# Other addresses for the stationary operands of a cross-attention, and value products that walk backwards

## The chip, the core and the metric

The kernel runs on one core of a Trainium2 chip. The metric is the device time of one execution in microseconds. Two runs of the kernel before took 585.60 and 587.18 us, median 586.39.

## What is computed

A block of 256 tokens (width 512) attends to 25,088 context rows, then runs a small causal self-attention and a mixture of eight experts. Nearly all of the time goes into the cross-attention:

```python
qp = einsum('bsd,ed->bse', q, Wq) + bq        # 256 x 128
kp = einsum('bsd,ed->bse', k, Wk) + bk        # 25088 x 128
vp = einsum('bsd,ed->bse', v, Wv) + bv        # 25088 x 512
z  = sigmoid(einsum('bqe,bke->bqk', qp, kp) / sqrt(128))
return einsum('bqk,bkd->bqd', z, vp)
```

There is no softmax, so the order can be turned round: the kernel sums z times the raw context rows, and multiplies the 256 x 512 result by Wv at the end (the bias bv enters with the row sums of z).

## The kernel before

**Numbers.** Each float32 operand of these products is split in two float32r parts, hi and lo (`split`, lines 62 to 65: ACT casts, DVE or POOL subtracts). `mm3` (lines 67 to 70) makes a product of three: hi x hi, hi x lo, lo x hi, added up in one bank of PSUM. The profile's lines L68, L69 and L70 are these three, wherever they are called from, so products are told apart by their tiles.

**Stationary and moving.** A product on TensorE has a stationary operand (`lhsT`, 128 columns here), which is loaded into the array first, and a moving operand (`rhs`), whose columns stream through. The profile shows the load as LDWEIGHTS on a row of its own, PEld, beside the running product on PE.

**The chunk loop.** The context comes in 49 chunks of 512 rows, each in two layouts: transposed (`rT`) and natural (`rN`), 1 MB each, loaded by SP's queue two or three chunks ahead. For each chunk:

- key products (`kp_mm`): stationary `wk` (four blocks j), moving the split transposed chunk T; 4 x 3 products of 512 columns
- scores (`scores`, two pairs of key tiles): stationary the chunk's `kp`, moving `qp`; 12 products of 256 columns. ACT applies the sigmoid, DVE adds z to its running sum, and z is split
- value products (`av`): for each of four key tiles t and two token halves q: stationary a 128 x 128 block of z, moving 512 columns of N (the split natural chunk), added up in `acc0` or `acc1`; 4 x 2 x 3 products of 512 columns

In TensorE's order the key products of the next chunk come first, then the value products of tiles 0 and 1, a score group of the next chunk, value products of tile 2, another score group, and those of tile 3. The order on each engine is the order of the program text (`in_order` fixes it). Beside this, `prepare` splits other weights and writes them to DRAM, a piece per chunk. After the loop come the 256-row stages, in a sequence written out by hand.

**Places in SBUF.** Tiles come from two pools, `sm` and then `sb`, placed one after the other in order of first request. In the program before, `half` is 41 columns wide instead of 1. All tiles in question begin at a multiple of 256 bytes, and so do the blocks taken from them: for every float32r product, stationary and moving operand lie at 0 modulo 256 bytes. `wk` are two tiles of 512 columns in `sb`; a `z` tile is [128, 2, 256], four buffers for each of hi and lo.

Of the kernel before, what the change touches and what calls it, by code (L numbers as in the profile page):

```python
# [11 lines left out]
F32 = mybir.dt.float32  # L12
F32R = mybir.dt.float32r
BF16 = mybir.dt.bfloat16
# [6 lines left out]
P = 128  # L21
T = 256
D = 512
KD = D // P
# [3 lines left out]
NT = CK // P  # L28
E = 8
NH = 16  # L30
LAG = 2
# [17 lines left out]
def body(ctx, tc, a, out, nch=NCH):  # L49
    nc = tc.nc  # L50
# [3 lines left out]
    sm = ctx.enter_context(tc.tile_pool(name="sm", bufs=1))  # L54
    sb = ctx.enter_context(tc.tile_pool(name="sb", bufs=1))
# [3 lines left out]
    def f(t):  # L59
        return t.bitcast(F32)  # L60

    def split(hi, lo, src, eng=nc.vector):

        copy(hi, src)  # L64
        eng.tensor_tensor(lo, src, f(hi), ALU.subtract)  # L65

    def mm3(ps, ahi, alo, bhi, blo, first, last):
        mm(ps, lhsT=ahi, rhs=bhi, start=first, stop=False)  # L68
        mm(ps, lhsT=ahi, rhs=blo, start=False, stop=False)  # L69
        mm(ps, lhsT=alo, rhs=bhi, start=False, stop=last)  # L70

    def pair(name, shape, tag=None, bufs=1):
        return [sb.tile(shape, F32R, tag=f"{tag or name}{i}", name=f"{name}_{i}", bufs=bufs) for i in range(2)]

    def bank(name):
        return psum.tile([P, D], F32, tag="b", name=name, bufs=6)
# [4 lines left out]
    def toks(t):  # L81
        return slice(t * P, (t + 1) * P)


    ident = sm.tile([P, P], F32, name="ident")
    make_identity(nc, ident)
    half = sm.tile([P, 41], F32, name="half")[:, 0:1]
    nc.gpsimd.memset(half, -0.5)
    ones = sm.tile([P, 1], F32, name="ones")
    nc.gpsimd.memset(ones, 1.0)  # L90
    x_sb = [sb.tile([P, D], F32, tag=f"x{t}", name=f"x_sb{t}") for t in range(2)]
    bq = sm.tile([P, 1], F32, name="bq")
    bk = sm.tile([P, 1], F32, name="bk")
    bv = sb.tile([P, D], F32, name="bv")
    rows = sm.tile([P, 2], F32, name="rows")
    zacc = sb.tile([P, 2, T], F32, name="zacc")
    nc.vector.memset(zacc, 0.0)
    wv = pair("wv", [P, KD * D], "wvo")
# [1 line left out]


    plain = {"wkvd": D, "wqr": 4 * 64, "wkr": 64, "wku": D, "wvu": D, "wq2": KD * D, "gate": KD * E}
    pw = {n: (sb if w % P == 0 else sm).tile([P, w], F32, name=n) for n, w in plain.items()}
    plain = list(pw)
    spill = {n: dram.tile([P, 2 * w], F32, name=f"sp_{n}") for n, w in (("wo", KD * D), ("gu", E * 2 * D), ("dn", E * D))}

    todo = [("wv", at, None, at) for at in range(0, KD * D, D)]
# [2 lines left out]
    todo += [("wo", at, KD * D, at) for at in range(0, KD * D, D)]  # L110


    mask = sm.tile([P, P], BF16, name="mask")
    nc.gpsimd.memset(mask, 0.0)
    nc.gpsimd.affine_select(out=mask, in_=mask, compare_op=ALU.is_ge, fill=MASKED, base=0, pattern=[[-1, P]],
                            channel_multiplier=1)
# [5 lines left out]
    def moments(x, tag):  # L122
        s6 = sm.tile([P, nc.vector.BN_STATS_DIM], F32, tag="s6", name=f"s6{tag}", bufs=2)
        mv = sm.tile([P, 2], F32, tag="mv", name=f"mv{tag}", bufs=2)
        rs = sm.tile([P, 1], F32, tag="rs", name=f"rs{tag}", bufs=2)
        nc.vector.bn_stats(s6, x)
        nc.vector.bn_aggr(mv, s6)
        nc.vector.tensor_scalar(rs, mv[:, 1:2], 1e-5, None, ALU.add)
        nc.gpsimd.tensor_tensor(rs, rs, half, ALU.pow)
        return mv, rs  # L130
# [12 lines left out]
    rT, rN, sT, sN, kp, zz = {}, {}, {}, {}, {}, {}  # L143
# [24 lines left out]
    def kp_mm(c, blocks=range(KD)):  # L168
        th, tl = sT[c]
        if c not in kp:  # L170
            kp[c] = bank(f"kp_ps{c}")
        ps = kp[c]
        for j in blocks:
            mm3(ps, wk[0][:, toks(j)], wk[1][:, toks(j)], th[:, j, :], tl[:, j, :], j == 0, j == KD - 1)

    def kp_out(c):
        ps, kp[c] = kp[c], pair(f"kp{c}", [P, CK], "kp", 2)
# [3 lines left out]
    def scores(c, p):  # L181
        ps = bank(f"sc{c}_{p}").rearrange("p (i t) -> p i t", i=2)
        for i in range(2):
            t = toks(2 * p + i)
            mm3(ps[:, i, :], kp[c][0][:, t], kp[c][1][:, t], qp[0], qp[1], True, True)
        z = sb.tile([P, 2, T], F32, tag="z", name=f"z{c}_{p}", bufs=2)
        nc.scalar.activation(z, ps, AF.Sigmoid, scale=1.0 / math.sqrt(128.0))  # L187
        zz[c, p] = pair(f"z{c}_{p}", [P, 2, T], "z", 2 * LAG)
        tt2(zacc, zacc, z, ALU.add)  # L189
        split(*zz[c, p], z)  # L190

    def av(c, t, q):
        zh, zl = zz[c, t // 2]
        nh, nl = sN[c]
        mm3(acc[q], zh[:, t % 2, toks(q)], zl[:, t % 2, toks(q)], nh[:, t, :], nl[:, t, :],
            c == 0 and t == 0, c == nch - 1 and t == NT - 1)

    def prepare(n):

# [12 lines left out]
    def load_split(n, tag):  # L212
        r = sb.tile([P, D], F32, tag="wr", name=f"{n}_r", bufs=2)
        nc.sync.dma_start(r, a[n])
        return r, pair(n, [P, D], tag)

    wk_r, wk = load_split("wk", "wk")
    for t in range(2):
        nc.sync.dma_start(x_sb[t], a["x"][:, t, :])
    wq_r, wq = load_split("wq", "at")  # L220
# [8 lines left out]

    acc = [psum.tile([P, D], F32, tag=f"acc{q}", name=f"acc{q}") for q in range(2)]  # L230
    xh, xl = pair("xa", [P, KD, T], "oh")
    warm = sm.tile([P, 1], F32, name="warm")
    nc.scalar.activation(warm, half, AF.Sigmoid)
    split(*wk, wk_r, nc.gpsimd)
    m = [moments(x_sb[tt], f"a{tt}") for tt in range(2)]
    xn = [normal(x_sb[tt], m[tt], f"xa{tt}") for tt in range(2)]
    split(*wq, wq_r, nc.gpsimd)
# [1 line left out]
    for j in range(2):  # L239
        split_T(0, [j])  # L240
        split(xh[:, :, toks(j)], xl[:, :, toks(j)], xps[j])
    split_T(0, [2, 3], nc.gpsimd)
    kp_mm(0, [0, 1])
    qp = pair("qp", [P, T])
    ps = bank("qp_ps")[:, :T]
    for j in range(KD):
        mm3(ps, wq[0][:, toks(j)], wq[1][:, toks(j)], xh[:, j, :], xl[:, j, :], j == 0, j == KD - 1)
    kp_mm(0, [2, 3])
    split_T(1, [0, 1])
    split_T(1, [2, 3], nc.gpsimd)  # L250
    nc.scalar.activation(qp[0], ps, AF.Identity, bias=bq)
    nc.vector.scalar_tensor_tensor(qp[1], ps, bq, f(qp[0]), ALU.add, ALU.subtract)
    kp_out(0)
    split_N(0, [0, 1])
    kp_mm(1, [0, 1])
    scores(0, 0)
    scores(0, 1)
    split_N(0, [2, 3])
    kp_mm(1, [2, 3])
# [3 lines left out]
    for c in range(nch):  # L263
# [23 lines left out]
        for t in range(NT):  # L287
            for q in now:
                av(c, t, q)
            if nx and t in (1, 2):  # L290
                scores(c + 1, t - 1)
        if c >= 4 and plain:
            n = plain.pop()
# [263 lines left out]
    def AV1(n):  # L557
        for _ in range(min(n, len(late))):
            av(*late.pop(0), 1)
# [5 lines left out]
    ps = bank("rows_ps")  # L565
# [54 lines left out]
    Q(1, 2)  # L620
    Q(1, 3)
    ft = sb.tile([P, 2 * D], F32R, tag="wq2", name="ft").rearrange("p (n b e d) -> p n b e d", n=2, b=2, e=2)
    fr, fq = (sb.tile([P, 2, 2, P], F32, tag=f"wk{i}", name=f"f{i}") for i in range(2))
    yhl = pair("y", [P, KD, T], "oh")
    PV(0, 2)
    PV(0, 3)
# [144 lines left out]
```

## Time and profile before

| | |
|---|---|
| median of the runs (2) | 586.39 us |
| profiled execution, its own time | 586.28 us |
| its span, first to last instruction | 584.5 us |
| granted TensorE clock | 1.00 |
| ACT cast of T, 128x2048 | 1.91 us |
| DVE subtraction for T, 128x2048 | 2.29 us |
| rT load of 1 MB, issue to landing | 5.5 us (median) |

How to read it: the busy row gives each engine's busy time; for TensorE the products overlap in the pipeline, so their lengths add up to more than the time that passes. The distance between two starts in the timeline is the pace. In a steady chunk, from 300.86 to 310.50 us, DVE is busy 8.25 us, ACT 7.37 us, and the DMA engines 86%:

```
us, PE busy (x) PEld busy (x) DVE busy (x) ACT busy (x) POOL busy (x), PEclk, DMA share, GB/s
300.86:310.50 9.64, 9.64 (x50) 8.19 (x48) 8.25 (x9) 7.37 (x8) 0.00 (x0) 1.00 0.86 306
```

The page's names for what the change touches: `kp_ps<-T,wk` (key products), `sc<-qp,kp` (scores), `acc<-N,z` (value products), `wk<-wk_r` (split of wk).

### The profile page before, as it was taken

To read this page: it belongs to the slowest core of one execution; us is meant where nothing else is said; L and a number is where in the kernel's file an instruction comes from. 1 tells how busy PE (TensorE), PEld (TensorE's weight loads), DVE (VectorE), ACT (ScalarE), POOL (GpSimd) and SP (SyncE) were. 2 spreads that over 40 slices of the span, in tenths; PEclk is the share of its full clock that TensorE was granted. 3 is DMA by queue.
4 is the path that set the end of the run, shared out by engine and by line. 5 is a ranking of instruction groups with operands and counts; after the bars stand their busy time and mean duration, and the time that the engine had idled before them with its cause. 6 is when DMAs were issued, how large, how long until landed. Compare 5 with 4: busy or idle time off the path is not lost.

```text
span 584.5 us, 8061 instructions
## 1 busy us (share of the span) xinstructions
PE 570.6 (98%) x3036; PEld 481.7 (82%) x3036; DVE 459.7 (79%) x528; ACT 395.1 (68%) x512; POOL 21.1 (4%) x28
## 2 busy tenths in 40 slices
PE   4999999999999999999999999999999999999997
PEld 3888888888888888888888888888888887876996
DVE  6898888888888888888888888787878765667543
ACT  5877777777777777777777776767676752574211
POOL 5200000000000000000000000000000041000000
PEclk9999999999999999999999999999999999999999
DMA  8897887879888888788988887565657477700000
GB/s 288 334 368 283 278 295 281 321 278 317 287 324 276 325 271 325 266 337 298 332 282 319 274 337 245 208 225 206 234 198 243 149 295 262 316 1 1 1 1 36
DMA packets 33526, 144.94 MB, mean 248 GB/s; under 512 B 4240, under 2 KB 4432, under 8 KB 19792
## 3 DMA queue, kind: packets, MB, share of 16 engines
q1 hardware_dynamic: 33488, 144.44, 69.3%
q8 instruction: 23, 0.38, 0.2%
q14 instruction: 15, 0.12, 0.1%
HBM read 129.22 MB, written 15.20 MB: 247 GB/s over the span
## 4 chain that ended last, share of the span: by engine, by line
PE 95%; DVE 3%; DMA 1%; issue 0%; POOL 0%; ACT 0%; SPq 0%; POOLq 0%
PE acc L68 15%; PE acc L69 15%; PE acc L70 15%; PE kp_ps L70 8%; PE kp_ps L69 8%; PE kp_ps L68 8%; PE sc L70 4%; PE sc L69 4%; PE sc L68 4%; PE s L428 2%; PE gu L68 1%; PE gu L69 1%; PE gu L70 1%; PE pt L445 1%; DMA wq_r<-in_wq 1%; PE pv L456 1%
## 5 line engine op out<-in xcount | busy, mean ns | idle before, releaser
L68 PE MATMUL acc<-N,z 128*128 128x512 f32 x392 | 153.9, 393 | 0.0
L69 PE MATMUL acc<-N,z 128*128 128x512 f32 x392 | 153.7, 392 | 0.0
L65 DVE TENSOR_TENSOR N<-rN,N 128x2048 fp32r<-128x2048 f32 (+1 forms) x53 | 111.6, 2110 | 52.3 <-ACT N L64 52.2
L70 PE MATMUL acc<-N,z 128*128 128x512 f32 x392 | 152.5, 389 | 0.0
L65 DVE TENSOR_TENSOR T<-rT,T 128x2048 fp32r<-128x2048 f32 (+1 forms) x49 | 110.3, 2252 | 15.3 <-ACT T L64 15.3
L187 ACT ACTIVATE z<-sc 128x512 f32<-128x512 f32 x98 | 58.7, 599 | 66.5 <-PE sc L70 66.2
L64 ACT CAST N<-rN 128x2048 fp32r<-128x2048 f32 (+1 forms) x55 | 94.4, 1725 | 6.1
L64 ACT CAST T<-rT 128x2048 fp32r<-128x2048 f32 (+1 forms) x55 | 94.3, 1721 | 0.9 <-DMA rT<-in_ctxT 0.7
L70 PEld LDWEIGHTS acc<-N,z 128*128 128x128 f32 x392 | 73.6, 188 | 16.0
L68 PEld LDWEIGHTS acc<-N,z 128*128 128x128 f32 x392 | 74.0, 189 | 12.3
L69 PEld LDWEIGHTS acc<-N,z 128*128 128x128 f32 x392 | 74.0, 189 | 11.7
L68 PE MATMUL kp_ps<-T,wk 128*128 128x512 f32 x196 | 76.9, 392 | 0.0
L70 PE MATMUL kp_ps<-T,wk 128*128 128x512 f32 x196 | 76.7, 392 | 0.0
L69 PE MATMUL kp_ps<-T,wk 128*128 128x512 f32 x192 | 74.7, 389 | 0.0
L189 DVE TENSOR_TENSOR zacc<-zacc,z 128x512 f32<-128x512 f32 x98 | 67.2, 686 | 3.7 <-ACT z L187 1.7
L65 DVE TENSOR_TENSOR z<-z,z 128x512 fp32r<-128x512 f32 x98 | 67.3, 686 | 0.0
L64 ACT CAST z<-z 128x512 fp32r<-128x512 f32 x98 | 61.0, 623 | 3.1
L178 ACT ACTIVATE kp<-kp_ps,bk 128x512 fp32r<-128x512 f32 x49 | 33.9, 691 | 39.9 <-PE kp_ps L70 39.9
L70 PE MATMUL sc<-qp,kp 128*128 128x256 f32 x196 | 55.8, 285 | 0.1
L69 PE MATMUL sc<-qp,kp 128*128 128x256 f32 x196 | 55.4, 283 | 0.0
L68 PE MATMUL sc<-qp,kp 128*128 128x256 f32 x196 | 54.9, 280 | 0.0
L68 PEld LDWEIGHTS kp_ps<-T,wk 128*128 128x128 f32 x196 | 37.1, 189 | 7.8
(177 smaller groups left out, 658.5 us busy)
## 6 DMA issues: line engine op xcount, KB each, us to landing
rN<-in_ctxN SPq DMA_DIRECT2D x49, 1024.0 KB, 5.7
rT<-in_ctxT SPq DMA_DIRECT2D x47, 1024.0 KB, 5.5
sp_gu<-w_gu SPq DMA_DIRECT2D x32, 256.0 KB, 4.3
gu<-sp_gu SPq DMA_DIRECT2D x8, 1024.0 KB, 6.0
r_gu<-in_gu SPq DMA_DIRECT2D x16, 256.0 KB, 5.7
sp_dn<-w_dn SPq DMA_DIRECT2D x16, 256.0 KB, 4.3
dn<-sp_dn SPq DMA_DIRECT2D x16, 256.0 KB, 6.0
r_dn<-in_dn SPq DMA_DIRECT2D x8, 256.0 KB, 6.1
```

The lines of the kernel that those rows point to most:

```text
L64: copy(hi, src)
L65: eng.tensor_tensor(lo, src, f(hi), ALU.subtract)
L68: mm(ps, lhsT=ahi, rhs=bhi, start=first, stop=False)
L69: mm(ps, lhsT=ahi, rhs=blo, start=False, stop=False)
L70: mm(ps, lhsT=alo, rhs=bhi, start=False, stop=last)
L178: nc.scalar.activation(kp[c][0], ps, AF.Identity, bias=bk)
L187: nc.scalar.activation(z, ps, AF.Sigmoid, scale=1.0 / math.sqrt(128.0))
L189: tt2(zacc, zacc, z, ALU.add)
L428: mm(p3[:, h - h0:h - h0 + 2, :], lhsT=qs[:, tt, h // 2, g, :], rhs=kbd[g // 2][:, g % 2, h:h + 2, :nk], start=tt == 1, stop=tt == 0 and h ...
L445: nc.tensor.transpose(ps[:, toks(i * (tt + 1) + kt)], pr[tt, u][:, i, toks(kt)], ident)
L456: mm(pv[tt][r, g, :], lhsT=vs[kt][:, g * P + r.start:g * P + r.stop], rhs=pt[tt, u][:, toks(i * (tt + 1) + kt)], start=kt == 0, stop=kt == tt)
```

## The change

Three things.

1. `wk` moves to `sm`, in two tiles of 568 columns; its four blocks begin at columns 4, 148, 292 and 436, so each lies 64 bytes further modulo 256 than the one before. It is split block by block.
2. A `z` tile gets 16 columns more, and z begins at column 4. With 2112 bytes a buffer, each of the four buffers lies 64 bytes further modulo 256.
3. `mm3` gets `back`: moving operand and output are read and written from the last column to the first. `av` sets it for odd key tiles.

The small tiles are requested in another order (`half` and `pad` 8 columns each), and `fr` and `fq`, which take the place of `wk` after the loop, become views of the wider tiles.

The addresses in the built programs, modulo 256 bytes:

| product | stationary before | moving before | stationary after | moving after | distance after |
|---|---|---|---|---|---|
| key, blocks j = 0 to 3 | 0 | 0 | 48, 112, 176, 240 | 64 | 240, 48, 112, 176 |
| value, by buffer of z | 0 | 0 | 16, 80, 144, 208 | 64 (backwards: from 60) | 208, 16, 80, 144 |
| scores | 0 | 0 | 64 | 64 | 0 |

```diff
-    def mm3(ps, ahi, alo, bhi, blo, first, last):
+    def mm3(ps, ahi, alo, bhi, blo, first, last, back=False):
+        if back:
+            ps, bhi, blo = ps[:, ::-1], bhi[:, ::-1], blo[:, ::-1]
         mm(ps, lhsT=ahi, rhs=bhi, start=first, stop=False)
...
+    ones, bq, bk, warm = [sm.tile([P, 1], F32, name=n) for n in ("ones", "bq", "bk", "warm")]
+    rows = sm.tile([P, 2], F32, name="rows")
+    mask = sm.tile([P, P], BF16, name="mask")
+    wkp = [None, None]
+    wkp[0] = sm.tile([P, D + 56], F32R, tag="wk0", name="wk0")
+    plain = {"wkr": 64}
+    pw = {n: sm.tile([P, w], F32, name=n) for n, w in plain.items()}
+    half = sm.tile([P, 8], F32, name="half")[:, 0:1]
+    wkp[1] = sm.tile([P, D + 56], F32R, tag="wk1", name="wk1")
+    pad = sm.tile([P, 8], F32, name="pad")
     ident = sm.tile([P, P], F32, name="ident")
     make_identity(nc, ident)
-    half = sm.tile([P, 41], F32, name="half")[:, 0:1]
...
-            mm3(ps, wk[0][:, toks(j)], wk[1][:, toks(j)], th[:, j, :], tl[:, j, :], j == 0, j == KD - 1)
+            mm3(ps, wk[0][j], wk[1][j], th[:, j, :], tl[:, j, :], j == 0, j == KD - 1)
...
-        zz[c, p] = pair(f"z{c}_{p}", [P, 2, T], "z", 2 * LAG)
+
+        zz[c, p] = [t[:, 4:2 * T + 4].rearrange("p (i t) -> p i t", i=2)
+                    for t in pair(f"z{c}_{p}", [P, 2 * T + 16], "z", 2 * LAG)]
...
-            c == 0 and t == 0, c == nch - 1 and t == NT - 1)
+            c == 0 and t == 0, c == nch - 1 and t == NT - 1, t % 2 == 1)
...
-    wk_r, wk = load_split("wk", "wk")
+    wk_r = sb.tile([P, D], F32, tag="wr", name="wk_r", bufs=2)
+    nc.sync.dma_start(wk_r, a["wk"])
+
+    wk = [[t[:, o:o + P] for o in (4, 148, 292, 436)] for t in wkp]
...
-    split(*wk, wk_r, nc.gpsimd)
+    for j in range(KD):
+        split(wk[0][j], wk[1][j], wk_r[:, toks(j)], nc.gpsimd)
...
-    fr, fq = (sb.tile([P, 2, 2, P], F32, tag=f"wk{i}", name=f"f{i}") for i in range(2))
+    fr, fq = (sm.tile([P, D + 56], F32, tag=f"wk{i}", name=f"f{i}")[:, 0:D].rearrange("p (b e d) -> p b e d", b=2, e=2)
+              for i in range(2))
```

More of the change, by code (lines that the diff above doesn't have):

```diff
@@ L82, in toks @@
         return slice(t * P, (t + 1) * P)
+    ones, bq, bk, warm = [sm.tile([P, 1], F32, name=n) for n in ("ones", "bq", "bk", "warm")]
[8 more added lines that the diff above has]
+    pad = sm.tile([P, 8], F32, name="pad")
     ident = sm.tile([P, P], F32, name="ident")
     make_identity(nc, ident)
-    half = sm.tile([P, 41], F32, name="half")[:, 0:1]
     nc.gpsimd.memset(half, -0.5)
-    ones = sm.tile([P, 1], F32, name="ones")
     nc.gpsimd.memset(ones, 1.0)
     x_sb = [sb.tile([P, D], F32, tag=f"x{t}", name=f"x_sb{t}") for t in range(2)]
-    bq = sm.tile([P, 1], F32, name="bq")
-    bk = sm.tile([P, 1], F32, name="bk")
     bv = sb.tile([P, D], F32, name="bv")
-    rows = sm.tile([P, 2], F32, name="rows")
     zacc = sb.tile([P, 2, T], F32, name="zacc")
@@ L102, in body @@
     plain = {"wkvd": D, "wqr": 4 * 64, "wkr": 64, "wku": D, "wvu": D, "wq2": KD * D, "gate": KD * E}
-    pw = {n: (sb if w % P == 0 else sm).tile([P, w], F32, name=n) for n, w in plain.items()}
-    plain = list(pw)
+    pw.update({n: (sb if w % P == 0 else sm).tile([P, w], F32, name=n) for n, w in plain.items() if n not in pw})
+    plain = list(plain)
     spill = {n: dram.tile([P, 2 * w], F32, name=f"sp_{n}") for n, w in (("wo", KD * D), ("gu", E * 2 * D), ("dn", E * D))}
@@ L110, in body @@
     todo += [("wo", at, KD * D, at) for at in range(0, KD * D, D)]
-    mask = sm.tile([P, P], BF16, name="mask")
     nc.gpsimd.memset(mask, 0.0)
@@ L231, in body @@
     xh, xl = pair("xa", [P, KD, T], "oh")
-    warm = sm.tile([P, 1], F32, name="warm")
     nc.scalar.activation(warm, half, AF.Sigmoid)
-    split(*wk, wk_r, nc.gpsimd)
+    for j in range(KD):
+        split(wk[0][j], wk[1][j], wk_r[:, toks(j)], nc.gpsimd)
     m = [moments(x_sb[tt], f"a{tt}") for tt in range(2)]
```

## The prediction, on record before the result

> **What bounds the kernel now.** I read the page first: the busy row and the chain of waits, then the groups by cost.
>
> ```profile
> span 584.5 us, 8061 instructions
> PE 570.6 (98%) x3036; PEld 481.7 (82%) x3036; DVE 459.7 (79%) x528; ACT 395.1 (68%) x512; POOL 21.1 (4%) x28
> PE 95%; DVE 3%; DMA 1%; issue 0%; POOL 0%; ACT 0%; SPq 0%; POOLq 0%
> L68 PE MATMUL acc<-N,z 128*128 128x512 f32 x392 | 153.9, 393 | 0.0
> ```
>
> TensorE is the chain: 95% of the span, and its groups have no idle time before them. No wait can be removed to any profit; only the pace of the products counts. The mean of 393 ns is the length of one product in flight and overlaps the next, so the pace has to be read from starts, in the timeline of TensorE. One turn of the chunk loop (300.86 to 310.50 us), with lines left out:
>
> ```profile
> 303.35 0.39 PE L70 MATMUL acc<-N,z 128*128 128x512 f32 x1
> 303.58 0.28 PE L68 MATMUL sc<-qp,kp 128*128 128x256 f32 x1
> ...
> 304.29 0.40 PE L68 MATMUL acc<-N,z 128*128 128x512 f32 x1
> ...
> 305.68 0.28 PE L68 MATMUL sc<-qp,kp 128*128 128x256 f32 x1
> ...
> 307.78 0.39 PE L68 MATMUL kp_ps<-T,wk 128*128 128x512 f32 x1
> ...
> 310.50 0.39 PE L68 MATMUL acc<-N,z 128*128 128x512 f32 x1
> ```
>
> The twelve key products take 307.78 to 310.50, so 226.7 ns each. The six score products (256 columns) take 0.71 us, 118 ns each. The six value products after a score group take 1.39 us, 231.7 ns each, five ns more than the twelve before 303.58. A chunk is 48 products in 9.64 us, and 49 chunks make 472 of the 584.5 us.
>
> How near is that to the least possible? Three products elsewhere in the trace answer, again by the distance of starts:
>
> ```profile
> 13.25 0.41 PE L69 MATMUL qp_ps<-xa,wq 128*128 128x256 f32 x1
> 13.46 0.41 PE L70 MATMUL qp_ps<-xa,wq 128*128 128x256 f32 x1
> ...
> 506.00 0.38 PE L426 MATMUL s<-mask,identb 128*128 128x512 bf16 x1
> 506.01 0.41 PEld L428 LDWEIGHTS s<-kbd,qs 128*128 128x128 f32 x2
> 506.22 0.38 PE L428 MATMUL s<-kbd,qs 128*128 128x256 f32 x1
> ...
> 513.10 1.06 PE L354 MATMUL q_ps<-xT,wq 128*128 128x128 f32 x8
> 513.99 0.38 PE L426 MATMUL s<-mask,identb 128*128 128x512 bf16 x1
> ```
>
> A 512-column bf16 product lets the next start after 0.22 us (216 ns in the trace's ns), although a float32 stationary operand is loaded beside it. At the start, at half pace, a 256-column float32r product takes 0.21 us, which is 256 columns at 1.2 per ns with nothing added. A plain float32 product of 128 columns comes every 0.89/8 = 111 ns, about the time of its load of 128 columns. So an excess of 226.7 - 216 = 10.7 ns stands only where float32r columns (4 bytes) move at full pace while a load of 4-byte columns runs beside them: 9.6 bytes/ns moving (2048 bytes in 213 ns) against 4.6 loading (512 in 111). It varies too: 114 ns for the first score product of a group and 120 for the later ones, 226.7 or 231.7 for value products of one shape. A fixed price per product would not do that. I read it as the two reads of SBUF disturbing each other. In the program before, every float32r operand lies at 0 modulo 256 bytes, so every distance is 0 and the trace can't show what a distance does.
>
> **What the Trainium skill says.** "TensorE: Matmul & The Clock Gate", section "Wait — 56ns, not 53.3ns?", gives N columns over 2.4 GHz plus about 2.5 ns: 215.7 for 512. The trace agrees for the bf16 product (216), not for float32r (226.7). Its section "Step-by-step: what each phase is for" says that TensorE has two independent read ports and that a load doesn't steal read bandwidth from the running product. If so, a distance can't matter; the 10.7 ns speak against it. "SBUF — State Buffer", section "Door 1: The DMA port swizzle", gives lines of 16 bytes in SBUF and 8 bytes in PSUM, and says that any non-contiguous access to PSUM slows products significantly. No product of before walks backwards, so the trace doesn't test whether a step of -1 counts as such.
>
> **The change part by part.** The order on every engine is as before, except that the split of wk is four casts and four subtractions instead of one each.
>
> *Distances.* 588 key products (49 x 12) and 1176 value products (49 x 24) get distances of 16, 48, ... 240 bytes. Scores keep 0. From both sides: at best the whole excess goes, 1764 x 10.7 = -18.9 us, and with it the extra after score groups, 2 x 6 x 5 ns x 47 chunks = -2.8. At worst it doubles: +18.9. For the value I take: in the 111 ns of a load the load walks 512 bytes and the moving operand 1024, so it gains 512 bytes, twice round 256, from whatever distance it starts. The number of meetings is two at every distance. I take 0.
>
> *Walking backwards.* 588 value products (odd tiles) read and write from the last column. Then the two walks go against each other: 1024 + 512 = 1536 bytes, six times round instead of two. Each meeting is a third as long. If a meeting costs by its length, 0; if each costs the same 5.35 ns, 6 x 5.35 instead of 10.7: +21.4 ns x 588 = +12.6 us. If the reversed order is refused the full pace, a product takes the 430 ns of a plain float32 one (two of them between 521.17 and 522.03): +203 x 588 = +119. Below nothing: at best its own excess goes, which is counted above. I take a quarter of the meeting price, +5.4 ns x 588 = +3.2 us.
>
> *Split of wk.* ACT: a cast of 128 columns isn't shown; between 128x1 (0.20) and 128x512 (0.62) it is about 0.31, so 1.22 instead of 0.62, ending near 4.6 us. ACT's next work, the cast of wq, waits for its DMA until 7.17: hidden. POOL: between 0.55 (one column) and 1.27, about 0.73 each, 2.9 instead of 1.27, from 3.7 to 6.6. Behind it on POOL stands rsa (5.34), which DVE needs at 7.04: with its 0.55 it ends near 7.15. At most +0.5 us; I take 0, since the second rsa starts at 7.20 anyway.
>
> *Moved addresses.* All other tiles start at 64 modulo 256 instead of 0, and each queue issues the same transfers in the same order. "DMA: Bandwidth & Descriptors", section "How a descriptor splits into AXI transactions", charges an unaligned start part of a transaction more. The cover: the rT load issued at 306.42 lands in about 5.5 us and is cast at 321.44, so 9.5 us are spare. If it were gone, ACT's cast of T would wait first. ACT and DVE do the same work on the same shapes; they are busy 7.4 and 8.3 of each 9.64 us. I take 0.
>
> *Sum.* 0 + 3.2 + 0 + 0 = +3.2 us on the profiled execution of 586.28 (span 584.5 and 1.8 around it), which stands at the median, 586.39: 589.5, rounded to **589**.
>
> **The rivals.**
> (a) Distance 0 is the bad one: stationary and moving walks start together, and an odd multiple of 16 bytes keeps them out of each other's lines. For it: the excess changes with the moment of the load (114 against 120). Against: two meetings at any distance. All of the excess and the extra: 586.3 - 18.9 - 2.8 = 565; half of it, 575. DVE's 8.3 us still fit under a chunk of 9.2.
> (b) Slower: distance 0 is the good one, because the walks start in one place and part at once, and other distances add a meeting in the middle of the load. Place: key and value products. Price: double excess, 1764 x 10.7 = +18.9, so 605. It decides from 6.7 ns per product (11.7 us, 2%), or 20 ns on the backward ones alone. For it: the first score product of a group costs 6 ns less than the later ones at distance 0, so cheaper states exist there.
> (c) Reversed columns lose the full pace: 586.3 + 119 = 705. For it: the skill's line on PSUM. Against: a pair of neighbours still fills an 8-byte line in either direction.
> (d) The change does nothing: the ports are independent and the 10.7 ns belong to float32r itself. 586. The varying gaps speak against it.
>
> **How the numbers follow.** The forecast (near-neutral, 583 to 596) 0.35, with (d) 0.10 more: 0.45 within 2% (574.7 to 598.1, about what a measurement of this kernel can tell from no change). (a) 0.20. (b), with the full price of meetings on the backward walk, 0.28, and (c) 0.07: 0.35 slower. The range reaches down to nearly all of (a), 567, and up past (b), 609; (c) and the ends of (a) and (b) are left out.
>
> **What would show it.** In the timeline of TensorE: key products still 226 to 228 ns apart and score products 120 (right: distance is neutral); backward value products 0 to 21 ns above forward ones of the same chunk. Key products near 216 mean (a), near 237 mean (b), backward ones near 430 (c). ACT waiting for rT would show that the transfers lost their cover. I am wrong if the pace of key products moves by more than 3 ns on average, or the backward ones by more than 10.

## The result, and the profile after

The kernel after takes 594.74 us (median of two runs, 594.24 to 595.23), against 586.39 before: a ratio of 1.0148, interval 1.0131 to 1.0164. The change costs 8.35 us, less than 2% but clearly more than nothing. The profiled execution took 594.24 us, 7.96 more than that of before, at the same granted clock of 1.00.

The page of the kernel after: span, busy row, shares of the chain, and the first group by cost (busy us and mean ns of one, then the idle time before it).

```profile
span 592.2 us, 8067 instructions
PE 578.9 (98%) x3036; PEld 481.3 (81%) x3036; DVE 459.6 (78%) x528; ACT 394.9 (67%) x515; POOL 21.6 (4%) x31
PE 94%; DVE 2%; DMA 1%; SPq 1%; issue 1%; ACT 0%; POOL 0%
L70 PE MATMUL acc<-N,z 128*128 128x512 f32 x392 | 155.3, 396 | 0.0
```

TensorE is still the chain and as full as before. It does the same 3036 products and is busy 8.3 us longer; DVE and ACT are within 0.2 us of before. No wait was added: the time is in the products. (`mm3` has moved down: L70, L71, L72 are now the three that were L68, L69, L70.) Busy time by stretch confirms the place. The first stretch is before, the second after, both from the first value product to the last:

```profile
20.90:492.60 471.70, 470.10 (x2340) 398.81 (x2339) 394.01 (x383) 347.50 (x378) 8.42 (x6) 1.00 0.79 279
```

```profile
20.60:500.30 479.70, 478.27 (x2340) 399.08 (x2339) 394.08 (x383) 347.12 (x378) 8.40 (x6) 1.00 0.77 276
```

The loop is 8.0 us longer, all of the difference of the profiled executions; what lies before and after it cost nothing. One turn in the timeline of TensorE, with lines left out (start, length):

```profile
282.91 0.39 PE L70 MATMUL kp_ps<-T,wk 128*128 128x512 f32 x1
...
285.69 0.40 PE L70 MATMUL acc<-N,z 128*128 128x512 f32 x1
...
287.09 0.39 PE L70 MATMUL acc<-N,z 128*128 128x512 f32 x1
...
288.51 0.28 PE L70 MATMUL sc<-qp,kp 128*128 128x256 f32 x1
...
289.23 0.40 PE L70 MATMUL acc<-N,z 128*128 128x512 f32 x1
...
290.62 0.28 PE L70 MATMUL sc<-qp,kp 128*128 128x256 f32 x1
```

Twelve key products take 2.78 us, so 231.7 ns each instead of 226.7. The six value products behind them (tile 0, forward) take 1.40 us, 233 each, and the six of tile 1 (backward) 1.42, 237. After a score group six more take 1.39 us, 232, as before. The six scores take 0.72, unchanged. Means over chunks 5 to 43, from start to start in ns; the experiments' rows belong to the next section:

| kernel | key | value forward | value backward | scores |
|---|---|---|---|---|
| before | 226.66 | 228.95 | | 118.77 |
| after | 231.24 | 233.44 | 233.93 | 118.93 |
| e1_fwd | 231.90 | 232.74 | | 118.73 |
| e2_back_d0 | 228.04 | 228.97 | 233.99 | 119.01 |
| e3_base64 | 226.66 | 228.99 | | 118.69 |
| e9_keys_alone | 230.69 | 230.00 | | 118.75 |
| e5_uni144 | 226.67 | 226.74 | | 118.75 |
| e12_scores176 | 226.66 | 229.34 | | 116.88 |

They add up: 588 x (4.58 key + 4.49 forward + 4.98 backward) = 2.7 + 2.6 + 2.9 = 8.3 us, the difference of the medians.

The columns mix two situations. By key tile, 0 to 3, the value products of before took 226.7, 226.7, 231.2 and 231.2 ns, those of after take 234.1, 234.6, 232.8 and 233.2. Nearly all of the loss falls on the keys and on tiles 0 and 1, which ran at 226.7; tiles 2 and 3, each behind a score group, were slow before and lose 2 ns.

### The profile page after: what moved, and what is told of

The parts are those of the page before. It is cut to its first block, busy times and chain, and to the rows that moved or that the text cites. A ratio compares the mean times of both kernels' runs of the same rounds, so it can differ in the third digit from the quotient of the medians.

```text
span 592.2 us, 8067 instructions
## 1 busy us (share of the span) xinstructions
PE 578.9 (98%) x3036; PEld 481.3 (81%) x3036; DVE 459.6 (78%) x528; ACT 394.9 (67%) x515; POOL 21.6 (4%) x31
## 4 chain that ended last, share of the span: by engine, by line
PE 94%; DVE 2%; DMA 1%; SPq 1%; issue 1%; ACT 0%; POOL 0%
PE acc L72 15%; PE acc L70 15%; PE acc L71 15%; PE kp_ps L70 7%; PE kp_ps L72 7%; PE kp_ps L71 7%; PE sc L72 4%; PE sc L71 4%; PE sc L70 4%; PE s L439 2%; PE gu L70 1%; PE gu L72 1%; PE gu L71 1%; DMA rT<-in_ctxT 1%; PE pt L456 1%; PE pv L467 1%
## 5 line engine op out<-in xcount | busy, mean ns | idle before, releaser
L72 PE MATMUL acc<-N,z 128*128 128x512 f32 x392 | 155.4, 397 | 0.0
L71 PE MATMUL acc<-N,z 128*128 128x512 f32 x392 | 155.4, 396 | 0.0
L70 PE MATMUL acc<-N,z 128*128 128x512 f32 x392 | 155.3, 396 | 0.0
L72 PEld LDWEIGHTS acc<-N,z 128*128 128x128 f32 x392 | 73.8, 188 | 17.8
L71 PEld LDWEIGHTS acc<-N,z 128*128 128x128 f32 x392 | 73.6, 188 | 13.5
L70 PEld LDWEIGHTS acc<-N,z 128*128 128x128 f32 x392 | 73.8, 188 | 12.9
L70 PE MATMUL kp_ps<-T,wk 128*128 128x512 f32 x196 | 78.0, 398 | 0.9 <-ACT T L64 0.9
L72 PE MATMUL kp_ps<-T,wk 128*128 128x512 f32 x196 | 77.5, 395 | 0.0
L71 PE MATMUL kp_ps<-T,wk 128*128 128x512 f32 x192 | 75.4, 392 | 0.0
L72 PE MATMUL sc<-qp,kp 128*128 128x256 f32 x196 | 55.6, 284 | 0.1
L71 PE MATMUL sc<-qp,kp 128*128 128x256 f32 x196 | 55.2, 282 | 0.0
L70 PE MATMUL sc<-qp,kp 128*128 128x256 f32 x196 | 55.0, 281 | 0.0
L70 PEld LDWEIGHTS kp_ps<-T,wk 128*128 128x128 f32 x196 | 37.2, 190 | 9.8 <-ACT T L64 1.3
```

## The experiments

All kernels below are compared with runs of the kernel before on the same chip.

### Which of the three parts costs: e1_fwd, e2_back_d0, e3_base64

e1_fwd is the kernel after, with every value product forward.

```diff
-            c == 0 and t == 0, c == nch - 1 and t == NT - 1, t % 2 == 1)
+            c == 0 and t == 0, c == nch - 1 and t == NT - 1, False)
```

> The changed kernel with every value product walking forwards; addresses as in the change. Theory D (the distances cost, about 5 ns on each of 1764 products, the direction costs nothing): 594 us, within 1 of the changed kernel, key products still 231 ns apart, value products of both kinds 233. Rival W (the backward walk costs, and throws the following products out of step): 588 us or less, key products back at 227. Rival B (the base address of 64 costs, neither of the two): 594 as well, to be told from D by the run with the base alone.

Measured: 594.18 us, 1.0141 [1.0124, 1.0159]. The distances without any backward walk cost as much as the whole change (594.74).

e2_back_d0 is the kernel before, with the backward walk for odd tiles and nothing else. The distances stay 0 (4 where the walk begins at the last column).

```diff
-    def mm3(ps, ahi, alo, bhi, blo, first, last):
+    def mm3(ps, ahi, alo, bhi, blo, first, last, back=False):
+        if back:
+            ps, bhi, blo = ps[:, ::-1], bhi[:, ::-1], blo[:, ::-1]
...
-            c == 0 and t == 0, c == nch - 1 and t == NT - 1)
+            c == 0 and t == 0, c == nch - 1 and t == NT - 1, t % 2 == 1)
```

> The kernel before with the odd key tiles walking backwards, all distances 0 (4 where a backward product runs beside a load). Theory D: 586 to 588 us, key products 227 ns apart. Rival W: 593 to 595 us. If the direction matters only because it changes the distance by 4 bytes, the backward products alone are slower, about 232, and the time is 589.

Measured: 589.84 us, 1.0064 [1.0047, 1.0082]. Its timeline of TensorE, from the last backward products of a chunk into the keys of the next:

```profile
308.87 0.40 PE L70 MATMUL acc<-N,z 128*128 128x512 f32 x1
...
310.27 0.40 PE L70 MATMUL kp_ps<-T,wk 128*128 128x512 f32 x1
310.51 0.39 PE L71 MATMUL kp_ps<-T,wk 128*128 128x512 f32 x1
310.74 0.39 PE L72 MATMUL kp_ps<-T,wk 128*128 128x512 f32 x1
310.97 0.39 PE L70 MATMUL kp_ps<-T,wk 128*128 128x512 f32 x1
```

The six backward products take 1.40 us, 233 each. The first two keys after them are 0.24 and 0.23 apart (238 and 232 in the trace's ns) although their operands lie as before; then the pace is 226 to 227 again. Backward costs 588 x 5.0 = 2.9 us, and the keys behind it 588 x 1.4 = 0.8: 3.7 of the 3.8 measured. Alone the walk costs something, beside the distances little: products of odd tiles average 232.3 ns in e1_fwd and 233.9 in the kernel after, and the two medians are 0.6 us apart.

e3_base64 moves every tile by 64 bytes, stationary and moving alike, so that they lie at 64 modulo 256 at distance 0.

```diff
-    half = sm.tile([P, 41], F32, name="half")[:, 0:1]
+    half = sm.tile([P, 57], F32, name="half")[:, 0:1]
```

> The kernel before with half 57 columns wide, so that every operand lies at 64 modulo 256 and all distances stay 0. Theory D and rival W: 586 us and the same gaps as before (227, 114 to 120, 226 to 236). Rival B: 592 to 595 us, key products 231 ns apart.

Measured: 586.12 us against 586.05, 1.0001 [0.9992, 1.0009]. Places that move together cost nothing: key products stay at 226.7 ns, and the loads of 1 MB still land in 5.5 us (rT) and 5.7 us (rN).

### Which distances: e4_survey16, e7_fine

e4_survey16 is the kernel before with another distance for every three chunks, 0 to 240 in steps of 16. The stationary operands of key and value products (wk, z) stay where they are and T and N move; for the scores kp moves.

```diff
...
-            sT[c] = [sb.tile([P, KD, CK], F32R, tag=tag, name=f"{tag}_{c}", bufs=n) for tag, n in (("T0", 2), lo)]
+            m = -off(c) % 64
+            sT[c] = [sb.tile([P, KD * CK + 64], F32R, tag=tag, name=f"{tag}_{c}", bufs=n)[:, m:m + KD * CK]
+                     .rearrange("p (j k) -> p j k", j=KD) for tag, n in (("T0", 2), lo)]
...
```

> The kernel before, all forward, with one distance for key, score and value products of a chunk, which is 0 in chunk 0 and then goes through 0, 16, 32, ... 240 bytes, three chunks each (T, N and kp tiles 64 columns wider, bv loaded after the loop). Theory D1 (a distance has a price of its own): key products of the later two chunks of each three lie between 216 and 240 ns and differ by distance, 0 being among the best and 48 and 112 near 233. Rival D2 (any constant distance settles at 227, only a change of distance or of product length costs, for about six products): all distances give 227 in the last chunk of three, and the extra stands only in the first products after a change. Rival D3 (odd multiples of 16 are bad, even ones good): two levels, 227 and 233, in turn.

Measured: 592.76 us in a single run. No distance is near 216, and none near 237 throughout. Two stretches of key products of this kernel, both at distance 16, one and the same code (the first key product of each, and the first value product behind the twelve):

```profile
56.91 0.40 PE L68 MATMUL kp_ps<-T,wk 128*128 128x512 f32 x1
...
59.71 0.40 PE L68 MATMUL acc<-N,z 128*128 128x512 f32 x1
...
66.74 0.40 PE L68 MATMUL kp_ps<-T,wk 128*128 128x512 f32 x1
...
69.58 0.40 PE L68 MATMUL acc<-N,z 128*128 128x512 f32 x1
```

The first twelve keys take 2.80 us, 233.3 each, the second twelve 2.84, 236.7. In the trace's ns from start to start:

```
distance 0,   steady   227 227 226 227 227 226 227 227 226 227 227 226
distance 16,  chunk 5  234 233 233 234 233 233 234 233 233 234 233 233
distance 16,  chunk 6  239 234 240 234 239 234 239 234 240 234 239 234
distance 144, chunk 29 234 231 237 225 231 237 225 231 238 225 231 237
distance 144, chunk 30 227 226 227 227 226 227 227 226 227 227 226 227
```

The excess isn't scattered: the products fall into a repeating pattern, and one pair of addresses can have two. Distance 0 gave 226.7, distance 144 too in its last chunk, and the other 42 chunks 228.8 to 236.7, a third of them within 0.1 of 233.3.

e7_fine leaves the kernel as it was and appends, after the output, 64 groups of 20 products of 512 columns, with distances 0 to 252 in steps of 4; their results go nowhere.

```diff
...
+        for i in range(times):
+            s = st[:, base + d // 4 + (i % 8) * 128:][:, :w]
+            mm(o, lhsT=s, rhs=m, start=i == 0, stop=i == times - 1)
+
+    for d in list(range(0, 256, 4)):
+        many(d)
```

> The kernel before and then, after its output, 64 groups of 20 products (512 columns, forward, operands that are in SBUF anyway) at distances 0, 4, 8, ... 252 bytes. Their results are not used. Theory of lines (two reads meet when they are in one 16-byte line of a 256-byte cycle): the mean gap is the same for the four distances within 16 bytes and steps between them. Rival (exact alignment counts): 227 at 0 alone, 231 to 234 at 4, 8 and 12. Rival D2 (any constant distance settles): all at 227 after six products. Under theory L a group may carry on the pattern of the one before it.

Measured, steady mean of a group: 226.7 at 0, 120, 132, 144, 156, 228 and 252; 228 to 238.8 at the rest, 233.3 at 29 of the 64. Neighbours 4 bytes apart differ (0: 226.7, 4: 232.4, 8: 230.6, 12 and 16: 233.3), so lines of 16 bytes that a load shares with the moving operand don't explain it alone; a group can also inherit from the one before it, as the next runs show.

### Whose excess it is: e8_width, e10_parts

e8_width appends groups of 20 at sixteen distances in four shapes: backward; stationary of 64 columns; of 32; moving of 256 columns.

```diff
...
+    for w, n, back in ((128, 512, True), (64, 512, False), (32, 512, False), (128, 256, False)):
+        for d in list(range(0, 256, 16)):
+            many(d, w, n, back)
```

> The kernel before and then, after its output, groups of 20 products at distances 0, 16, ... 240: backward with 512 columns, forward with stationary operands of 64 and of 32 columns, and forward with 256 moving columns. Their results are not used. If the excess over 213 ns comes from the load's reads, it shrinks with the load: 227 to 233 at 128 columns, about 217 to 223 at 64, 215 to 218 at 32. If it belongs to the product itself, 227 to 233 at every width. Backward products: 233 to 234 at every distance (theory: against each other the walks never settle), or 227 at one of them (the direction only moved the distance by 4 bytes).

Groups by cost of this kernel, shapes apart:

```profile
L721 PEld LDWEIGHTS bench<-gu,gu 128*128 128x128 f32 x640 | 98.0, 188 | 14.9
L721 PE MATMUL bench<-gu,gu 128*128 128x512 f32 x320 | 75.0, 398 | 0.0
L721 PE MATMUL bench<-gu,gu 128*32 128x512 f32 x320 | 74.2, 394 | 0.0
L721 PE MATMUL bench<-gu,gu 128*64 128x512 f32 x320 | 73.9, 393 | 0.0
L721 PEld LDWEIGHTS bench<-gu,gu 128*32 128x32 f32 x320 | 34.6, 108 | 39.4
```

Divide busy time by count for the pace: 234 ns backward with a load of 128 columns, and forward 231 with 64 and 232 with 32. The forward groups of e7_fine with 128 columns, at the same sixteen distances, average 231.6. The load record falls from 188 to 108 ns and the excess over 213 ns (512 columns at 2.4 per ns, the full pace of which the prediction's 1.2 was half) doesn't fall with it. If the excess were time in which the load holds up the moving operand, a quarter of the load would have left a quarter of it.

e10_parts appends groups that take one of the two walks away: the moving operand stands still (one column read 512 times), the stationary one does, both do, bf16 instead of float32r; and others at distance 0 but other addresses.

```diff
...
+        m = x[:, lo + at // u:][:, 0:1].broadcast_to([P, D]) if still else x[:, lo + at // u:][:, 0:D]
...
+            s = s[:, 0:1].broadcast_to([P, P]) if hold else s[:, 0:P]
```

> The kernel before and then, after its output, groups of 20 products of 512 columns whose results are not used: distance 0 at eight addresses; the moving operand standing still (one column read 512 times); the stationary operand's columns all the same; both; bf16 operands; one stationary block for all 20; and distances 0, 16, 112, 144 in different orders. Theory R (two reads of SBUF that walk meet): with the moving operand standing still the distances differ no more, and the excess over 216 ns goes or becomes equal; bf16 216. Theory F (a fixed price of float32r at full pace, and the distance only sets when it falls): 227 to 233 with either operand standing still, bf16 216. Distance 0 gives 227 at all eight addresses if the distance alone counts. A distance that follows another one keeps its own pattern (no memory), or 16 and 112 give different patterns after different predecessors (memory).

| group | ns per product |
|---|---|
| moving stands still, distances 0, 16, 64, 144 | 218.7 at each |
| moving and stationary stand still | 218.7 |
| stationary stands still, same distances | 226.7 to 231.7 |
| bf16, same distances | 216 at each |
| distance 0, moving at 0, 32 | 226.7 |
| distance 0, moving at 4, 8, 12, 16, 100, 144 | 237.8, 231.2, 228.9, 233.3, 237.8, 231.2 |
| one stationary block for all 20, distances 0, 16, 64, 144 | 226.7, 226.7, 233.3, 233.3 |
| distance 16 after a group at 0; after a group at 64 | 226.7; 233 |
| distance 144 after a group at 226.7; after one at 233 | 226.7; 233 |

Where the moving float32r columns stand still the distance is without effect and 8 ns are gone, though the output is written as in the other groups. That alone would fit two walks that meet as well. But the distance keeps its effect where the load reads one place, and a load of a quarter of the columns (e8_width) leaves the excess as it is; these two don't fit. So the excess needs a moving operand of distinct 4-byte columns, and a count of meetings doesn't set it. It also has a memory: the same product is fast or slow by what ran before. Distance 0 at moving address 0 always comes back to 226.7, within ten products. The pace of the group before doesn't decide alone: in e7_fine the group at 144 goes at 226.7 from its first product, right behind one at 233.3.

### Is 144 as good as 0: e5_uni144, e11_144_scores

e5_uni144 puts key, value and score products at distance 144, in the kernel before (for key and value products stationary at 0, moving at 112); bv, which has no room beside the wider tiles, is loaded after the loop.

```diff
...
+            m = -144 // 4 % 64
...
+        o = 144 // 4
+        ps, kp[c] = kp[c], [t[:, o:o + CK] for t in pair(f"kp{c}", [P, CK + 64], "kp", 2)]
```

> The kernel before, all forward, with a distance of 144 bytes for key, score and value products in every chunk (in the survey this distance fell into even steps of 227 ns in its third chunk, value products after a score group included; bv loaded after the loop). Theory L (227 is one settled pattern among several, and which one is reached depends on the distance and on what went before; 144 holds it even across score groups): 583 to 584 us, value products after scores at 227 instead of 231. Rival: at 144 the pattern of the first two chunks (225, 231, 237 in turn, mean 231.8) comes back, 591 to 593 us. Rival D1 (a price per distance): the same as the mean of its three chunks in the survey, about 589.

Measured: 583.91 us against 586.58, 0.9949 [0.9930, 0.9968]: faster than both kernels of the change. One turn in its timeline:

```profile
300.03 0.39 PE L68 MATMUL acc<-N,z 128*128 128x512 f32 x1
...
303.46 0.39 PE L68 MATMUL acc<-N,z 128*128 128x512 f32 x1
...
304.82 0.28 PE L68 MATMUL sc<-qp,kp 128*128 128x256 f32 x1
...
309.61 0.39 PE L68 MATMUL acc<-N,z 128*128 128x512 f32 x1
```

The six value products after a score group take 1.36 us, 226.7 each, instead of 1.39; a turn takes 9.58 us instead of 9.64. Here a score group no longer throws the value products out of the fast pattern. The kernel isn't in this pattern from the start: the keys of chunk 2 go at 231.1, and in chunk 3 a stall of 0.16 us inside a score group throws the products out again. What follows:

```profile
44.08 0.33 PE L70 MATMUL sc<-qp,kp 128*128 128x256 f32 x1
44.24 0.28 PE L68 MATMUL sc<-qp,kp 128*128 128x256 f32 x1
...
44.60 0.39 PE L68 MATMUL acc<-N,z 128*128 128x512 f32 x1
...
45.98 0.28 PE L68 MATMUL sc<-qp,kp 128*128 128x256 f32 x1
...
46.69 0.39 PE L68 MATMUL acc<-N,z 128*128 128x512 f32 x1
...
48.05 0.39 PE L68 MATMUL kp_ps<-T,wk 128*128 128x512 f32 x1
```

The six value products behind the stall take 1.38 us, 230 each, and the six behind the next score group 1.36, 226.7 again. Both times the fast pattern came back directly behind a score group at 144.

e11_144_scores keeps key and value at 144 and steps the distance of the scores, to see what a score group leaves behind.

```diff
-        o = 144 // 4
+        o = DS[c] // 4
```

> Key and value products at distance 144, the score products' distance stepped through 144, 160, ... 128, three chunks each. Theory L: the key and value products stay at 227 for some score distances and are pushed to 231 to 233 for others; at a score distance of 64 the scores take 113 to 115 ns instead of 119 (113.3 in the long row), which would be 2 to 3 us over all chunks if value products stay at 227. Theory D1: value products at 227 whatever the scores' distance.

Measured: 590.83 us in a single run. A stall came first, in a score group of chunk 3, the last chunk with its scores at 144:

```profile
43.34 0.28 PE L69 MATMUL sc<-qp,kp 128*128 128x256 f32 x1
43.45 0.38 PE L70 MATMUL sc<-qp,kp 128*128 128x256 f32 x1
43.67 0.28 PE L68 MATMUL sc<-qp,kp 128*128 128x256 f32 x1
```

After this gap of 0.22 us the keys go at 231.1 (237, 225, 231 in turn) and don't come back at any of the other fifteen distances of the scores, so what each of these does to a settled pattern stayed unanswered. Earlier, with the scores at 144, the same kernel had come back from that very pattern, in chunk 1, as e5_uni144 did twice and e4_survey16 once, each time directly behind a score group at 144. So at 144 the key and value products keep the fast pattern but, in these runs of the loop, didn't find it by themselves; a score group at 144 can bring it back, though not every one does. That e5_uni144 recovers from every disturbance isn't shown: four runs were faster, and the one trace has two returns.

### What one group leaves to the next: e6_scores, e12_scores176, e9_keys_alone

e6_scores steps the scores alone, key and value at 0 (in this run and the next, too, bv is loaded after the loop).

> The kernel before, all forward, key and value products at distance 0, and only the score products' distance stepped through 0, 16, ... 240, three chunks each. Theory L: the key products stay at 227 in all chunks, the six value products after a score group change with the score distance (231 at 0), since scores are what pushes them out of the pattern. Theory D1: value products after scores stay at 231 whatever the score distance, and scores alone change, to 115 at distance 64 as in the survey.

Measured: 586.26 us in a single run. Keys stay at 226.7 (227.7 at a score distance of 48); the value products after a score group take 228.2 to 233.8 by the scores' distance, 231.2 at 0. I read a value of 228.2 as that of 176, and e12_scores176 put 176 in every chunk:

```diff
...
-        ps, kp[c] = kp[c], pair(f"kp{c}", [P, CK], "kp", 2)
+        o = 176 // 4
+        ps, kp[c] = kp[c], [t[:, o:o + CK] for t in pair(f"kp{c}", [P, CK + 64], "kp", 2)]
...
```

> Key and value products at distance 0, the score products at 176 (kp written 176 bytes further), bv loaded after the loop. Theory L (distance 0 settles by itself at 227; a score distance of 176 pushes the value products behind the scores out of it less far, 228.2 instead of 231.3, and takes 116.8 instead of 118.8 itself): 12 x 2.0 + 12 x 3.0 = 60 ns a chunk, 2.9 us in 48 chunks: 583 to 584 us. Rival (the survey's chunks owed this to what went before them): 585.5 to 587.

Measured: 585.53 us against 586.09, 0.9987 [0.9981, 0.9994]. The scores themselves go at 116.9 instead of 118.8 (588 x 1.9 = 1.1 us less); the value products after them take 231.6, and all value products together lose 1176 x 0.4 = 0.5 us of it again. The 228.2 was never the survey's value for 176. The scores of a chunk run among the value products of the chunk before, and the reading was one chunk late. In the trace's ns, the six value products behind the first score group and the six behind the second:

```
e6,  scores of chunk 35, at 176   231 233 236 224 231 236   231 231 236 228 232 231
e12, scores of chunk 46, at 176   231 233 236 224 231 236   231 231 236 228 232 231
e6,  scores of chunk 37, at 192   233 231 226 227 227 225   232 231 227 226 227 227
```

The survey's three chunks at 176 carried over product by product, so the time fell in the rival's range without the rival's reason. The low values belong to 144 and 192 (228.2 to 228.3 behind both score groups) and 208 (229.0 and 228.3). A turn at 192 takes 9.59 us instead of 9.64, an estimated 2 us over the loop; no run put 192 in every chunk with the keys and values at 0.

e9_keys_alone has the change's places for wk, and z at distance 0, all forward.

```diff
...
-        zz[c, p] = [t[:, 4:2 * T + 4].rearrange("p (i t) -> p i t", i=2)
-                    for t in pair(f"z{c}_{p}", [P, 2 * T + 16], "z", 2 * LAG)]
+        zz[c, p] = [t[:, 0:2 * T].rearrange("p (i t) -> p i t", i=2)
+                    for t in pair(f"z{c}_{p}", [P, 2 * T], "z", 2 * LAG)]
...
```

> The change's distances on the key products alone (240, 48, 112, 176 by block); value products at distance 0 and forward. If the parts add up (key products +5 ns on 588, in the run with all distances forward 231.9 against 226.7): +3.1 us, 589 to 590 us. If the value products are thrown out of the settled pattern by the key products before them, up to six of the twelve behind them rise to 231 to 235 as well: +1.5 more, 590.5 to 591.5. If the key products' distances cost nothing alone: 586.

Measured: 589.56 us, 1.0053 [1.0035, 1.0071]. Keys 230.7: 588 x 4.0 = 2.4 us. The value products behind them, at distance 0, need six to settle (231, 236, 228, 233, 231, 226, then 227): on average 1.05 more, x 1176 = 1.2. Together 3.6 us, 3.2 measured. Part of what slow products cost is paid by the good ones behind them.

### Address or distance: e13_map

It appends pairs of groups: ten products at stationary and moving address 0 (which settles at 226.7) or at 4 (237.8), and then 16 at each of 32 pairs of addresses.

```diff
...
+    for first in ((0, 0), (4, 4)):
+        for a in (0, 16, 32, 64):
+            for b in (0, 16, 32, 64, 112, 144, 176, 240):
+                many(*first, 10)
+                many(a, b, 16)
```

> The kernel before and then, after its output, 64 pairs of groups: ten products from a fixed start (moving and stationary operand both at 0, which settles at 227, or both at 4, which does not), then sixteen with the moving operand at 0, 16, 32 or 64 and the stationary one at 0, 16, 32, 64, 112, 144, 176 or 240. Results not used. Theory L: equal pairs (distance 0) reach 227 from either start where the moving operand is at 0, 32 or 64; other distances reach it from the settled start at some (16, 144) and from the other start rarely. Theory D1 (a price per distance): the last six gaps depend on the distance alone, whatever the start and the address. Rival A (the moving operand's address alone decides): rows of one moving address are equal, all 227 at 0, 32 and 64.

Mean ns of the later products of a group, for 13 of the 32 pairs:

| moving, stationary | from settled | from unsettled |
|---|---|---|
| 0,0 and 32,32 and 64,64 | 226.6 to 228.1, ending at 227 | 226.6 to 228.1, ending at 227 |
| 16,16 | 230.0 | 231.1 |
| 0,16 and 0,144 | 226.7 | 233.3 |
| 0,240 | 226.7 | 226.7 |
| 32,176 (distance 144) | 233.2 | 233.4 |
| 64,112 (distance 48) | 233.4 | 233.4 |
| 64,176 (distance 112) | 233.2 | 233.4 |
| 64,240 (distance 176) | 230.0 | 230.0 |
| 64,16 (distance 208) | 231.6 | 232.1 |
| 64,144 (distance 80) | 232.0 | 232.4 |

The last five rows are pairs of the change. They lie at 230 to 233 whatever ran before: with the moving operand at 64 none of them finds 226.7, and its key products, a mixture of four distances, went at 231.2. Distance alone isn't enough to say (0,144 and 32,176 differ). Two pairs that the table leaves out reached 226.7 from one start and not from the other: 16,112 from settled, 32,16 from unsettled.

## Why the prediction was right or wrong

**What bounds the kernel: right.** TensorE bound the kernel before and after (95% and 94% of the chain), only the pace counted, and the whole difference was found in the starts of the products of the chunk loop.

**The distances, taken at 0: wrong, the step that failed.** "The number of meetings is two at every distance. I take 0." Keys went 4.6 ns slower and value products 4.5 forward and 5.0 backward, 8.3 us in all, where the sum had 0 + 3.2. By its own mark (3 ns on the average key product) the prediction is wrong. e1_fwd, the distances without the walk, cost 8.1 alone. 8.3 us is inside the bound of 18.9, at 44% of it: the range held because it left room for the unknown, and the sign of the forecast was luck, since the sum had it from the walk. The step failed one sentence earlier, where the 10.7 ns were read as "the two reads of SBUF disturbing each other". That reading makes the count of meetings the price, and it falls: the excess doesn't shrink with a load of a quarter of the columns, and it stays when the load reads one place. The count of two also rested on a load of 111 ns, read from the pace of plain float32 products; the load records beside 512-column float32r products last 188. What the runs show in its place are patterns: distance 0 is where keys and tiles 0 and 1 settled at 226.7, and the new address pairs keep them at 231 to 235. The caution that stood beside it, that the trace of before shows distance 0 alone, was the better guide: the excess was known at one point, and a value for eight other points wasn't to be had from it.

**Walking backwards, +5.4 ns a product: the size right alone, the sum wrong.** e2_back_d0 shows +5.0 on the backward products and 3.8 us in all, of which 0.8 falls on the keys behind. But it doesn't add to the distances: e1_fwd, without it, takes 594.18, the whole change 594.74. Both lift a product out of the 226.7 pattern into those near 233, and once out it loses little more. The "quarter of the meeting price" behind the number has no support in the runs.

**Full pace for reversed columns, rival (c): refused.** Backward products take 234 ns, not 430. The Trainium skill's warning on "SBUF — State Buffer", section "Door 1: The DMA port swizzle", that non-contiguous access to PSUM slows products significantly, isn't borne out for a step of -1: 5 ns of 229 (2%) in the kernel.

**Rival (b), distance 0 is the good one: right in kind, half its price.** It named the place (key and value products) and the sign. Price 605, measured 594.7; it decides from 6.7 ns per product, and 4.7 came. Its reason (walks that start in one place and part at once) goes with the meetings. Distance 0 is good because the products settle into the 226.7 pattern there by themselves, and that with the moving operand at 0, 32 or 64, not at 4, 8, 12, 16, 100 or 144.

**Rival (a), distance 0 is the bad one: refused.** No distance gave a key or value product of the loop a steady pace under 226.7. What could be had was the extra after score groups, which the prediction had at 2.8 us: e5_uni144 gained 2.7.

**Rival (d) and the skill's ports.** "TensorE: Matmul & The Clock Gate", section "Step-by-step: what each phase is for", has the load not stealing bandwidth from the product. The runs agree so far as e8_width and the standing load go; no run takes the load away. The prediction drew from it that "a distance can't matter", which doesn't follow: addresses matter, whatever the load takes. The same page's 215.7 ns for 512 columns holds for bf16 (216), not for any float32r group with distinct columns.

**Split of wk and moved addresses: hidden, as predicted, the sizes too high.** The starts of ACT and POOL after the change:

```profile
3.53 0.90 ACT L64 CAST wk<-wk_r 128x128 fp32r<-128x128 f32 x4 [1.30 <-DMA wk_r<-in_wk]
6.93 0.62 ACT L64 CAST wq<-wq_r 128x512 fp32r<-128x512 f32 x1 [2.51 <-DMA wq_r<-in_wq]
```

```profile
3.91 1.69 POOL L65 TENSOR_TENSOR wk<-wk_r,wk 128x128 fp32r<-128x128 f32 x4 [1.92 <-ACT wk L64]
5.55 0.56 POOL L135 TENSOR_TENSOR rsa<-rsa,half 128x1 f32<-128x1 f32 x1
```

Four casts end at 4.43 and ACT then waits 2.51 us for wq's transfer, the cover that was named; POOL's four take 1.69 us instead of the 2.9 worked out, and rsa follows at 5.55. e3_base64 confirms that addresses which all move together cost nothing.

**What stays open.** Which part of TensorE or of SBUF makes these patterns isn't shown. What is shown: the excess needs distinct float32r columns that move, the addresses of both operands choose the patterns on offer, and what ran before chooses among them. The common paces are 213.3 + 2 x 6.7 and 213.3 + 3 x 6.7 ns, that is 32 and 48 columns' time (at 2.4 per ns) above 512; why they are 16 apart no run here tested. Nor did one test whether the excess is absent at the pace of the kernel's start, where 256 columns took 213 ns (the trace gives a granted clock of 1.00 there). The backward walk was tried in the kernel at distance 0 or 4 and in groups after it, not at other moving addresses.

## What to carry to other kernels

Where the products of a matmul-bound kernel are float32r, read their pace from start to start and look for a repeating pattern: 227 or 233 ns for 512 columns is decided by the addresses of both operands and by what ran before, and a rearrangement of the pools can move it by up to 3% with no wait to show for it. Keep stationary and moving operands at the same place modulo 256 bytes, at 0, 32 or 64, where products of 512 columns with loads of 128 came back to 226.7 by themselves, unless a run of the whole kernel shows a better choice (144 for all three kinds of product gained 2.7 us). A survey of a few chunks needs care twice: a pattern can be inherited from what ran before, and in a software pipeline the products behind a group belong to another chunk than the group. And where the trace shows an effect at a single setting, a mechanism read out of it gives no value for other settings: carry the bound, not the zero.

## What was not expected of the hardware

- The pace of a float32r product depends on history: 16 bytes of distance gave 233.3 and 236.7 in neighbouring chunks, and 226.7 or 233 after different groups.
- A group at distance 0 that is thrown out comes back by itself in about six products (e9_keys_alone); at distance 144 key and value products of the loop didn't, and came back only behind a score group at 144 (e5_uni144, e11_144_scores).
- 256 moving columns behave alike: 113.3 ns (distance 64) to 120.0 in e8_width, and scores at 116.9 instead of 118.8 by their address alone.
- A backward product costs 5 ns, and leaves the next two out of step, which costs 16.6 ns more per chunk in e2_back_d0 (238 and 232 instead of 226.7 twice).
